# Three edits to a two-layer adaptive transformer on one core: tokens issued before weights, an output projection moved into the next row, a softmax scale moved to ScalarE

## The chip, the cores and the metric

The kernel runs on one core of a Trainium2 chip. Its time is the device time of one execution in microseconds. Before the change the median of three runs is 4261.57 us (4254.47 to 4265.86). All data are float32 except a few small helper tiles.

## The reference

Input `x` has 8 rows of 512 tokens with 256 channels. Cut to what matters, it goes through four residual branches:

```python
x = x + ssm(adaln(x))          # layer 0: a gate from eight causal averages, then a selective state-space scan
x = x + moe2(x @ W[id7] + b)   # layer 0: 8 experts, top 2, gelu, hidden 512
x = x + attention(lora_ffn(x)) # layer 1: 8 heads of width 64, values 256 wide, softmax over 512 tokens
x = x + moe4(adapter_ln(x))    # layer 1: 32 experts, top 4, swiglu, hidden 128, plus a shared expert
```

with, inside them,

```python
h = exp(dlt * A) * h + dlt * B_t * x_t        # 512 channels x 16 states, 512 steps in order
y = (C_t . h + D * x_t) * silu(z); out = y @ W_out.T
attn = softmax(Q @ K.T); out = attn @ V       # per head, summed over heads
```

In both expert layers each token goes to its best experts only, and the experts' outputs are summed with the gate's weights.

## The kernel before

A row is kept as 128 partitions x 2 halves of the channels x 512 tokens. Two Python generators write the program in turns: one for the first branch (`thread_x`), one for the second and third (`thread_y`). They yield costs, and a loop at the end lets the first advance in proportion to the second. The rows go through the second generator in four groups: row 0; rows 1 and 2; rows 3 to 5; rows 6 and 7. What is written is then ordered once more, at build time, by a list scheduler: it keeps the dependencies, takes the earlier written instruction where several are ready by its own cost figures, gives out buffers as they come free, and puts each copy written as `nc.any` on VectorE or ScalarE, whichever it holds to be free. [...]

*The scan* (`scan`, L612 to L687). A row has 64 items: 4 channel blocks `j` x 4 groups of states `g` x 4 quarters `k`. For an item ScalarE makes `dA` (L623), GpSimd `h` (L625), VectorE scans (L651) and multiplies by C (L652), and TensorE folds the states into `yp` (L660). After each channel block, VectorE adds the skip term (L664) and GpSimd multiplies by the gate into the tile `y8` (L665). When the 64 items are written, the output projection follows (L680 to L686): load the row's input as `xr`, eight products of `y8` with `W_out` into two PSUM tiles `gx` (of which there are two in all), add, store to `xa`. While the items are written, the head of the next row (gates, causal averages, convolution) is woven in by the generator's loop (L703 to L709), which then marks the row as done. Done rows let the second generator start on a group.

*The first expert layer* (L780 to L812). Tokens were scattered by GpSimd into a table in HBM, sorted by expert, in tiles of 256. For a tile, SyncE reads the expert's and the tile's numbers into registers, and issues two loads: the expert's weights `fw` (1154 KB, 4 buffers) and the tokens `xt` (260 KB, 4 buffers), the latter behind a fence on the scatters. Then TensorE transposes the tokens (L298), ScalarE copies them (L300), two products with a gelu between them follow, VectorE adds the bias into `ys` (L808), works out where the rows go (`to_m`, `to_d`, `to_i`, L306 to L310), and GpSimd scatters them (L160). Tiles are written one step apart: transposes of one, first product of the one before it, second product of the one before that.

*Attention* (L862 to L927). Per pair of heads and per 128 queries, `scores` writes the products of queries and keys, the negated maximum on VectorE (L893), the exponential with its sum on ScalarE (L896), the sum's reciprocal on VectorE (L897) and the scaling:

```python
nc.scalar.activation(ex, sp, AF.Exp, bias=nm, accum_out=den)
nc.vector.reciprocal(den, den)
nc.vector.tensor_scalar(ex, ex, den, None, ALU.mult)
```

`turn` transposes the scaled tiles on TensorE (L906) and copies them (L907, an `nc.any` copy, as are those of V at L879 and of queries and keys at L871); the products with V follow (L923).

*The last expert layer* (L1060 to L1086) has the same form as the first, with weights `mw` (384 KB), tokens of 264 KB, 7 buffers of each and 95 tiles, after everything else. A gather per row ends the program.

Of the kernel before, what the change touches and what calls it, by code (L numbers as in the profile page):

```python
# [10 lines left out]
F32 = mybir.dt.float32  # L11
# [6 lines left out]
P = 128  # L18
# [33 lines left out]
def adaln_attn_ffn_kernel(ctx: ExitStack, tc: tile.TileContext, d: dict, out: bass.AP):  # L52
# [314 lines left out]
    def thread_x(wp, wk, ps):  # L367
# [244 lines left out]
        def scan(b):  # L612

            bc3 = rows[b]
            items = [(j, g, k) for j in range(4) for g in range(4) for k in range(4)]
            yps, Cs, hs, dAs, xz = {}, {}, {}, {}, {}
            y8 = wk.tile([P, 4, T], F32, tag="y8", name="y8")

            def begin(i):
                j, g, k = items[i]  # L620
                t = got[b, j, k]
                dA = wk.tile([P, T], F32, tag="dA", name="dA", bufs=4)
                nc.scalar.activation(dA, t[:, 0, :], AF.Exp, scale=A[:, 4 * j + k, g : g + 1])  # L623
                h = wk.tile([P, T], F32, tag="h", name="h", bufs=8)
                nc.gpsimd.tensor_tensor(h, t[:, 1, :], B4s[b, g], ALU.mult)  # L625
                hs[i], dAs[i] = h, dA
                if (g, k) == (1, 0):
                    xz[j] = wk.tile([P, 2, T], F32, tag="xz", name="xz")
                    nc.sync.dma_start(xz[j], xzs[b % 2][:, j])
                if j == 0 and g < 3 and k == 1:  # L630
                    get_B4(b, g + 1)

                if j < 3 and (g, k) == (2, 3):
                    get_pack(b, j + 1, 0)
                if j < 3 and g == 3 and k < 3:
                    get_pack(b, j + 1, k + 1)
                if j == 3 and b + 1 < NB and g == 3:
                    if k == 0:
                        get_pack(b + 1, 0, 0)
                    if k < 3:  # L640
                        get_pack(b + 1, 0, k + 1)
                    if k == 3:
                        get_B4(b + 1, 0)

            def run(i):
                j, g, k = items[i]
                h = hs[i]
                if k == 0:
                    Cs[0] = ps.tile([P, T], F32, tag="c4", name="c4")
                    mm(Cs[0], [(states(4 + g), bc3)])  # L650
                nc.vector.tensor_tensor_scan(h, dAs.pop(i), h, 0.0, ALU.mult, ALU.add)  # L651
                nc.vector.tensor_tensor(h, h, Cs[0], ALU.mult)  # L652

            def add(i):

                j, g, k = items[i]
                if g == 0:
                    yps[j] = ps.tile([P, T], F32, tag="yp", name="yp")
                for k in range(4):
                    nc.tensor.matmul(  # L660
                        yps[j][32 * k : 32 * k + 32, :], fold, hs.pop(i + k), start=(g == 0), stop=(g == 3))
                if g == 3:
                    y = wk.tile([P, T], F32, tag="tr", name="y", bufs=2)
                    nc.vector.scalar_tensor_tensor(y, xz[j][:, 0, :], col("D", j), yps.pop(j), ALU.mult, ALU.add)  # L664
                    nc.gpsimd.tensor_tensor(y8[:, j, :], xz.pop(j)[:, 1, :], y, ALU.mult)  # L665

            begin(0)
            begin(1)
            for i in range(64):
                if i == 58:  # L670
                    yield from after[0]
                if i < 62:
                    begin(i + 2)
                run(i)
                if i % 4 == 0 and i > 0:
                    add(i - 4)
                if i % 2:
                    yield 5
            add(60)
            x = wk.tile([P, KC, T], F32, tag="gm", name="xr")  # L680
            nc.sync.dma_start(x, d["x"][b])
            for e in range(KC):
                pt = gx()
                mm(pt, [(W_out[:, j, ts(e, P)], y8[:, j, :]) for j in range(4)])
                nc.vector.tensor_tensor(x[:, e, :], x[:, e, :], pt, ALU.add)
            nc.sync.dma_start(xa[b], x)  # L686
            yield 3  # L687

        after = [None]
        for i, c in enumerate(head_a(0)):  # L690
            if i == 14:
# [10 lines left out]

        for b in range(NB):  # L703
            after[0] = head(b + 1) if b + 1 < NB else iter(())
            for c in scan(b):
                c += next(after[0], 0)
                c += next(after[0], 0)
                yield c
            done.add(b)  # L709

    def thread_y(q, bs, ps):
        n = len(bs)
# [9 lines left out]
        with ExitStack() as ph:  # L722
# [57 lines left out]
            def expert_tile(i):  # L780
                with behind(last[-3] if i > 2 else None):
                    te = nc.sync.value_load(tiles[0:1, i : i + 1], min_val=0, max_val=E2 - 1)
                    v = nc.sync.value_load(tiles[0:1, NT + i : NT + i + 1], min_val=0, max_val=E2 * cap // TS - 1)
                    w = wk.tile([P, FW], F32, tag="fw", name="fw", bufs=4)
                    nc.sync.dma_start(w, d["fW"][bass.ds(te, 1)].rearrange("s p f -> p (s f)"))
                    xt = wk.tile([P, 2, RW2], F32, tag="xt", name="xt", bufs=4)
                    last.append(load_after(
                        f, xt.rearrange("p j f -> p (j f)"), tabv[bass.ds(v, 1)].rearrange("s p f -> p (s f)")))
                yield 0
                xT = tokens_in(wk, acc, xt, 2)  # L790
                yield 1
                h = wk.tile([P, FC, TS], F32, tag="h", name="h2")
                for hh in range(2):
                    pt = g()
                    for i2 in range(2):
                        fc = 2 * hh + i2
                        mm(pt[:, ts(i2, TS)],
                           [(w[:, 512 * k + P * fc : 512 * k + P * (fc + 1)], xT[:, k, :]) for k in range(KC)])
                    for i2 in range(2):
                        fc = 2 * hh + i2  # L800
                        nc.scalar.activation(h[:, fc, :], pt[:, ts(i2, TS)], AF.Gelu, bias=w[:, 2304 + fc : 2305 + fc])  # L801
                yield 4
                py = acc()
                for j in range(2):
                    mm(py[:, ts(j, C)],
                       [(h[:, fc, ts(j, P)], w[:, 1024 + C * fc : 1024 + C * (fc + 1)]) for fc in range(FC)])
                ys = wk.tile([P, 2, C], F32, tag="ys", name="ys", bufs=3)
                nc.vector.tensor_tensor(ys, py.rearrange("p (j c) -> p j c", j=2), rep(w[:, 2048:2304], 2), ALU.add)  # L808
                tokens_out(wk, xt, ys, teb[:, i : i + 1], K2, tok, n * T * K2, f"tok2_{q}")
                yield 4  # L810
# [4 lines left out]
        with ExitStack() as ph:  # L815
            wk = ph.enter_context(tc.tile_pool(name=f"k3_{q}", bufs=1))
            H = 8
            for r, b in enumerate(bs):
# [43 lines left out]
                for hp in range(H // 2):  # L862
# [20 lines left out]
                    def scores(i):  # L883

                        sps = [g() for u in range(2)]

                        for u in (1, 0):
                            r0 = 64 * u
                            mm(sps[u], [(qk[r0 : r0 + 64, 0, ts(i, P)], qk[r0 : r0 + 64, 1, :])])
                        for u in range(2):  # L890
                            sp = sps[u]
                            nm = wk.tile([P, 1], F32, tag="nm", name="nm", bufs=4)
                            nc.vector.tensor_reduce(nm, sp, AX.X, ALU.max, negate=True)  # L893
                            ex = wk.tile([P, T], F32, tag="ex", name="ex", bufs=NEX)
                            den = wk.tile([P, 1], F32, tag="den", name="den", bufs=4)
                            nc.scalar.activation(ex, sp, AF.Exp, bias=nm, accum_out=den)  # L896
                            nc.vector.reciprocal(den, den)  # L897
                            nc.vector.tensor_scalar(ex, ex, den, None, ALU.mult)  # L898
                            exs[i, u] = ex

                    def turn(i):
# [100 lines left out]
    with ExitStack() as ph:  # L1002
# [57 lines left out]
        def expert_tile(i):  # L1060
            with behind(last[-5] if i > 4 else None):
                te = nc.sync.value_load(rows[0:1, i : i + 1], min_val=0, max_val=E4 - 1)
                v = nc.sync.value_load(rows[0:1, NT + i : NT + i + 1], min_val=0, max_val=E4 * CAP4 // TS - 1)
                w = wk.tile([P, 768], F32, tag="mw", name="mw", bufs=7)
                nc.sync.dma_start(w, d["mW"][bass.ds(te, 1)].rearrange("s p f -> p (s f)"))
                xt = wk.tile([P, 2, RW4], F32, tag="xt", name="xt", bufs=7)
                last.append(load_after(
                    f, xt.rearrange("p j f -> p (j f)"), tab4v[bass.ds(v, 1)].rearrange("s p f -> p (s f)")))
            yield 1
            xT = tokens_in(wk, ps_tile, xt)  # L1070
            yield 1
# [130 lines left out]
```

## Time and profile before

| | us |
|---|---|
| median of the runs | 4261.57 |
| the profiled execution | 4252.41 |
| its span, first to last instruction | 4250.6 |
| TensorE busy | 3440.5 |
| VectorE busy | 2670.9 |
| ScalarE busy | 1672.2 |
| GpSimd busy | 1565.8 |
| mean granted TensorE clock | 0.889 of full speed |

The profile names engines PE (TensorE products), PEld (TensorE weight loads), DVE (VectorE), ACT (ScalarE), POOL (GpSimd) and SP (SyncE, which issues the loads); "q" after a name is the engine's sequencer. Busy times come from one execution. [...] A line of the list of waits tells that an engine stood idle ahead of an instruction and what ended that; idle time of an engine that nothing waits for costs nothing. Scan rows end (last VectorE scan) at 395, 718, 1047, 1393, 1738, 2064, 2579 and 2903 us; the first-layer expert tiles of the four groups lie at about 482 to 655, 1149 to 1380, 2188 to 2390 and 3135 to 3279; the last layer's run from 3827 to about 4160, and the gather ends the span.

### The profile page before, as it was taken

How to read it: one execution, taken by the hardware profiler on the slowest of the kernel's cores; microseconds unless marked ns; L12 is line 12 of the kernel's file. 1: busy time of each engine (PE TensorE's matmuls, PEld its weight loads, DVE VectorE, ACT ScalarE, POOL GpSimd, SP SyncE). 2: the span in 40 equal slices, each digit the busy share in tenths (PEclk: the TensorE clock that was granted, in tenths of full speed). 3: DMA queues.
4: the chain of work that ended last, by engine and by line, in shares of the span. 5: the costliest groups of instructions: out<-in, count | busy, mean ns of one | idle time of the engine just before them, and what ended most of it. 6: DMA issues, size and time to landing. Idle time of an engine off the chain costs nothing. (4 is left out here: it accounts for less than half of the span.)

```text
span 4250.6 us, 36891 instructions
## 1 busy us (share of the span) xinstructions
PE 3440.5 (81%) x10964; PEld 1694.3 (40%) x10964; DVE 2670.9 (63%) x4290; ACT 1672.2 (39%) x2741; POOL 1565.8 (37%) x1222
## 2 busy tenths in 40 slices
PE   4556686887687888888758899889988999978994
PEld 2111352332254233333327443333456444436773
DVE  4698957886966686796892547575432454443336
ACT  2535463455366346445433443242223233322222
POOL 0456535434635333433542323231043111134552
PEclk7677798988798898999879999899989999989996
DMA  3235455324456423333346312213043312117776
GB/s 105 101 108 180 187 162 170 106 98 156 177 176 209 135 102 118 134 122 109 139 165 234 122 63 77 68 36 104 15 163 136 93 41 70 36 50 245 248 237 224
DMA packets 159372, 554.78 MB, mean 131 GB/s; under 512 B 27730, under 2 KB 34289, under 8 KB 146756
## 3 DMA queue, kind: packets, MB, share of 16 engines
q1 hardware_dynamic: 135076, 501.35, 35.2%
q0 software_dynamic: 24096, 51.08, 3.3%
q8 instruction: 87, 1.43, 0.1%
q14 instruction: 113, 0.93, 0.1%
HBM read 453.00 MB, written 234.82 MB: 162 GB/s over the span
## 5 line engine op out<-in xcount | busy, mean ns | idle before, releaser
L625 POOL TENSOR_TENSOR h<-packed,B 128x512 f32<-128x512 f32 x512 | 792.5, 1570 | 1054.2 <-PE yp L660 746.7
L651 DVE TENSOR_TENSOR_SCAN h<-dA,h 128x512 f32<-128x512 f32 x512 | 791.0, 1571 | 126.3 <-ACT dA L623 67.2
L623 ACT ACTIVATE dA<-packed,Aexp 128x512 f32<-128x512 f32 x512 | 359.8, 720 | 656.4 <-DVE h L651 446.5
L160 POOL DMA_INDIRECT tok<-ys,to_i x310 | 311.9, 1006 | 497.9 <-DVE ys L808 237.7
L660 PE MATMUL yp<-h,fold 128*32 128x512 f32 x1024 | 349.7, 704 | 156.9 <-DVE h L652 140.6
L923 PE MATMUL acc<-aT,V 128*128 128x512 f32 x1024 | 453.4, 597 | 5.3 <-ACT aT L907 3.2
L160 POOL DMA_INDIRECT tab<-row,si x192 | 197.4, 1028 | 465.5 <-issue 210.5
L652 DVE TENSOR_TENSOR h<-h,c 128x512 f32<-128x512 f32 x512 | 330.5, 672 | 29.0 <-PE c L78 28.2
L923 PEld LDWEIGHTS acc<-aT,V 128*128 128x128 f32 x1024 | 193.2, 191 | 245.9 <-issue 235.1
L78 PE MATMUL acc<-wv,c 128*128 128x512 f32 x512 | 270.2, 642 | 0.4
L78 PE MATMUL g<-qk 64*128 64x512 f32 x512 | 210.7, 681 | 54.9 <-ACT ex L896 28.6
L896 ACT ACTIVATE ex<-g,nm 128x512 f32<-128x512 f32 x256 | 173.8, 684 | 157.5 <-DVE nm L893 157.3
L78 PE MATMUL g<-xT,fw 128*128 128x256 f32 x960 | 233.6, 396 | 2.5 <-ACT h L801 1.9
L893 DVE TENSOR_REDUCE nm<-g 128x1 f32<-128x512 f32 x256 | 165.0, 681 | 100.8 <-PE g L78 100.8
L78 PE MATMUL acc<-fw,h 128*128 128x256 f32 x960 | 221.6, 383 | 3.5 <-DVE ys L808 1.8
L78 PEld LDWEIGHTS g<-xT,fw 128*128 128x128 f32 x960 | 188.0, 201 | 39.4 <-issue 6.8
L78 PEld LDWEIGHTS acc<-fw,h 128*128 128x128 f32 x960 | 182.7, 192 | 41.6 <-issue 12.4
L906 PE MATMUL acc<-ident,ex 128*128 128x128 f32 x1024 | 160.3, 286 | 47.9 <-DVE ex L898 16.2
L906 PEld LDWEIGHTS acc<-ident,ex 128*128 128x128 f32 x1024 | 122.6, 146 | 188.4 <-issue 69.3
L660 PEld LDWEIGHTS yp<-h,fold 128*32 128x32 f32 x1024 | 44.7, 115 | 364.1 <-DVE h L652 208.3
L479 DVE TENSOR_TENSOR_SCAN tr<-alpha,gm 128x512 f32<-128x512 f32 x128 | 181.4, 1435 | 5.0 <-POOL y L665 3.5
L78 PE MATMUL g<-xT,mw 128*128 128x256 f32 x760 | 183.1, 385 | 0.0
(280 smaller groups left out, 5458.3 us busy)
## 6 DMA issues: line engine op xcount, KB each, us to landing
fw<-in_fW SPq DMA_DIRECT2D x60, 1154.0 KB
tab<-zeros SPq DMA_DIRECT2D x32, 2112.0 KB
packed<-pack SPq DMA_DIRECT2D x128, 512.0 KB
mw<-in_mW SPq DMA_DIRECT2D x95, 384.0 KB
tab<-zeros SPq DMA_DIRECT2D x16, 2080.0 KB
xt<-tab SPq DMA_DIRECT2D x95, 264.0 KB
xz<-xzs SPq DMA_DIRECT2D x32, 512.0 KB
pack<-dd SPq DMA_DIRECT2D x32, 512.0 KB
```

The costliest lines, as they stand in the source:

```text
L78: nc.tensor.matmul(o, lhsT, rhs, start=(i == 0), stop=(i == len(pairs) - 1))
L160: i = nc.gpsimd.indirect_dma_start(out=table_, out_offset=bass.IndirectOffsetOnAxis(ap=idx, axis=0), in_=src, in_offset=None, bounds_check ...
L479: nc.vector.tensor_tensor_scan(tr, alpha[:, 1 + i : 2 + i].to_broadcast([P, T]), gm[:, k, :], 0.0, ALU.mult, ALU.add)
L623: nc.scalar.activation(dA, t[:, 0, :], AF.Exp, scale=A[:, 4 * j + k, g : g + 1])
L625: nc.gpsimd.tensor_tensor(h, t[:, 1, :], B4s[b, g], ALU.mult)
L651: nc.vector.tensor_tensor_scan(h, dAs.pop(i), h, 0.0, ALU.mult, ALU.add)
L652: nc.vector.tensor_tensor(h, h, Cs[0], ALU.mult)
L660: nc.tensor.matmul(yps[j][32 * k : 32 * k + 32, :], fold, hs.pop(i + k), start=(g == 0), stop=(g == 3))
L893: nc.vector.tensor_reduce(nm, sp, AX.X, ALU.max, negate=True)
L896: nc.scalar.activation(ex, sp, AF.Exp, bias=nm, accum_out=den)
L906: nc.tensor.transpose(tp[:, m, :], ex[:, ts(m, P)], ident)
L923: nc.tensor.matmul(ys[k], V[:, m, C * u + P * k : C * u + P * (k + 1)], aTs[u][:, m, :], start=(u == 0 and m == 0), stop=(u == 1 and m == 3))
```

## The change

There are three edits. In both expert layers the tokens are issued before the weights:

```diff
-                    w = wk.tile([P, FW], F32, tag="fw", name="fw", bufs=4)
-                    nc.sync.dma_start(w, d["fW"][bass.ds(te, 1)].rearrange("s p f -> p (s f)"))
                     xt = wk.tile([P, 2, RW2], F32, tag="xt", name="xt", bufs=4)
                     last.append(load_after(
                         f, xt.rearrange("p j f -> p (j f)"), tabv[bass.ds(v, 1)].rearrange("s p f -> p (s f)")))
+                    w = wk.tile([P, FW], F32, tag="fw", name="fw", bufs=4)
+                    nc.sync.dma_start(w, d["fW"][bass.ds(te, 1)].rearrange("s p f -> p (s f)"))
...
-                w = wk.tile([P, 768], F32, tag="mw", name="mw", bufs=7)
-                nc.sync.dma_start(w, d["mW"][bass.ds(te, 1)].rearrange("s p f -> p (s f)"))
                 xt = wk.tile([P, 2, RW4], F32, tag="xt", name="xt", bufs=7)
                 last.append(load_after(
                     f, xt.rearrange("p j f -> p (j f)"), tab4v[bass.ds(v, 1)].rearrange("s p f -> p (s f)")))
+                w = wk.tile([P, 768], F32, tag="mw", name="mw", bufs=7)
+                nc.sync.dma_start(w, d["mW"][bass.ds(te, 1)].rearrange("s p f -> p (s f)"))
```

A row's output projection is written after the first items of the next row's scan instead of at its own row's end; the last row's stays behind its scan. The row counts as done when its projection has been written, the head of the row after next is woven in from the third turn on, and `y8` is taken when the first channel block is finished:

```diff
-            y8 = wk.tile([P, 4, T], F32, tag="y8", name="y8")
...
                 if g == 3:
+                    if j == 0:
+                        ys8[b % 2] = wk.tile([P, 4, T], F32, tag="y8", name="y8")
+                    y8 = ys8[b % 2]
...
                 if i < 62:
                     begin(i + 2)
+                if i == 2 and last:
+                    last.pop()()
                 run(i)
...
             add(60)
-            x = wk.tile([P, KC, T], F32, tag="gm", name="xr")
-            nc.sync.dma_start(x, d["x"][b])
-            for e in range(KC):
-                pt = gx()
-                mm(pt, [(W_out[:, j, ts(e, P)], y8[:, j, :]) for j in range(4)])
-                nc.vector.tensor_tensor(x[:, e, :], x[:, e, :], pt, ALU.add)
-            nc.sync.dma_start(xa[b], x)
-            yield 3
-
+            yield 0
+
+            def project():
+                x = wk.tile([P, KC, T], F32, tag="gm", name="xr")
+                nc.sync.dma_start(x, d["x"][b])
+                for e in range(KC):
+                    pt = gx()
+                    mm(pt, [(W_out[:, j, ts(e, P)], ys8[b % 2][:, j, :]) for j in range(4)])
+                    nc.vector.tensor_tensor(x[:, e, :], x[:, e, :], pt, ALU.add)
+                nc.sync.dma_start(xa[b], x)
+                done.add(b)
+
+            last.append(project)
+
+        last, ys8 = [], {}
...
-            for c in scan(b):
-                c += next(after[0], 0)
-                c += next(after[0], 0)
+            for i, c in enumerate(scan(b)):
+                if i > 1:
+                    c += next(after[0], 0)
+                    c += next(after[0], 0)
                 yield c
-            done.add(b)
+        last.pop()()
+        yield 3
```

The exponentials of the attention are scaled on ScalarE:

```diff
                             nc.vector.reciprocal(den, den)
-                            nc.vector.tensor_scalar(ex, ex, den, None, ALU.mult)
+                            nc.scalar.activation(ex, ex, AF.Identity, scale=den)
```

As the change is built, the scheduler's choices move along: of the `nc.any` copies of attention, VectorE has 176 where it had 121 (of 448), and ScalarE's order holds 299 loads of function tables where it held 286.

## The prediction

> **What bounds the kernel now.** I read the shares of the engines first, then the stretches of time, because an average over 4250 us hides stages with different limits. Columns of the second fence: stretch, length, busy us of each engine (instructions), granted TensorE clock, DMA share, GB/s.
>
> ```profile
> PE 3440.5 (81%) x10964; PEld 1694.3 (40%) x10964; DVE 2670.9 (63%) x4290; ACT 1672.2 (39%) x2741; POOL 1565.8 (37%) x1222
> ```
>
> ```profile
> 0.00:410.00 410.00, 232.16 (x419) 64.07 (x421) 306.47 (x314) 168.82 (x217) 176.13 (x121) 0.73 0.37 122
> 410.00:2940.00 2530.00, 2063.30 (x6317) 947.09 (x6313) 1798.24 (x2457) 1144.31 (x1822) 1019.30 (x725) 0.89 0.38 132
> 2940.00:3840.00 900.00, 821.28 (x2674) 428.78 (x2675) 382.25 (x943) 252.94 (x485) 185.48 (x185) 0.95 0.25 83
> 3840.00:4160.00 320.00, 288.21 (x1427) 233.73 (x1426) 124.33 (x448) 86.33 (x179) 171.14 (x176) 0.99 0.76 240
> 4160.00:4251.00 91.00, 35.50 (x132) 20.65 (x131) 59.59 (x130) 19.80 (x40) 13.70 (x15) 0.59 0.63 231
> ```
>
> There are five stages. Until 410 row 0 of the scan runs alone, led by VectorE (75% busy). From 410 to 2940 scan rows 1 to 7 are woven with the expert layer and attention of rows 0 to 5: TensorE is 82% busy, VectorE 71%, and neither is full; [...] From 2940 to 3840 (rows 6 and 7 with the last routing) TensorE is 91% busy and simply the limit. From 3840 the 95 last expert tiles run at 90% TensorE. The tail is the gather. So time can be won at TensorE's waits, most of all in the woven stage. The third fence is the list of waits: who waited for whom, us in total, times, longest.
>
> ```profile
> PE acc L298 <- DMA xt<-tab: 48.2, 22, 9.0
> PE gx L78 <- POOL y L665: 24.4, 8, 8.5
> PE acc L906 <- DVE ex L898: 16.2, 11, 5.1
> DVE to_m L306 <- DMA xt<-tab: 178.4, 32, 14.8
> SPq L785 <- DVE ys L808: 355.6, 43, 21.4
> ```
>
> TensorE waits 48.2 us for tokens and 24.4 us for the gated scan output ahead of the output projection; VectorE stands 178.4 us in front of the tokens. The timeline of one steady first-layer expert tile shows how the token wait arises (start, length, engine, line, idle before):
>
> ```profile
> 3166.43 0.69 DVE L808 TENSOR_TENSOR ys<-acc,fw 128x512 f32<-128x512 f32 x1
> ...
> 3167.25 0.34 SPq L785 DMA_DIRECT2D fw<-in_fW  x1
> ...
> 3167.78 0.33 SPq L179 DMA_DIRECT2D xt<-tab  x1
> ...
> 3173.69 0.22 DVE L306 SCALAR_TENSOR_TENSOR to_m<-xt,sc_teb 128x4 f32<-128x4 f32 x1 [6.57 <-DMA xt<-tab]
> ...
> 3173.80 0.63 PE L298 MATMUL acc<-ident,xt 128*128 128x128 f32 x4 [0.27 <-DMA xt<-tab]
> ```
>
> It is a ring: `ys` frees a weight buffer (3167.12), weights and tokens are issued, the tokens land 5.9 us after their issue because 1154 KB go first, and the transposes, the next `ys` and the next release follow. It turns in 7.8 us; TensorE's work for a tile is 3.62 + 3.62 + 0.63 = 7.87 us of modelled spans, so ring and engine are about equal. The waits at a row's end and the scaling:
>
> ```profile
> 1062.45 3.78 PE L78 MATMUL gx<-y,W_out 128*128 128x512 f32 x4 [8.47 <-POOL y L665]
> ```
>
> ```profile
> L898 DVE TENSOR_SCALAR ex<-ex,den 128x512 f32<-128x512 f32 x256 | 161.8, 634 | 3.3
> ```
>
> ```profile
> L623 ACT ACTIVATE dA<-packed,Aexp 128x512 f32<-128x512 f32 x512 | 359.8, 720 | 656.4 <-DVE h L651 446.5 <-DMA packed<-pack 132.2 <-issue 15.1
> ```
>
> [...]
>
> **The change, part by part.** The profiled execution took 4252.4 us, 1.8 more than its span; the median is 4261.6, 9.2 above it. Sums are made against 4252.4 and moved up by 9.2.
>
> *Tokens before weights, first layer (60 tiles).* The same two transfers change places. The tokens' buffer is freed by `to_m` and the transposes, long before `ys` frees the weights'. So tile i+1's tokens go out right behind tile i's weights, about one tile (7.8 us) earlier than they are needed, and leave the ring. The weights come 0.5 to 1 us later, and TensorE wants them only one step after the transposes (the first product follows the transposes of the next tile), so 7.9 us of TensorE work hides them; if that cover were gone, each tile would lose about 1 us, 60 in all. Late next is TensorE itself. Of the 48.2 us, 8.4 lie in the last group (3135 to 3280), where nothing else can fill TensorE: worth 8 in full. The other 40 lie in the woven stage, where TensorE's freed time is partly taken by other waits: I count half, 20. Bounds: 8 and 48, and something beyond for VectorE's 84 us of token waits in the first groups, behind which scans queue. SyncE's wait for `ys` (355.6 us) stays, with the scan's loads behind it as before.
>
> *Last layer (95 tiles).* With 7 buffers nothing waits for tokens in the steady stage; its 31.8 us of TensorE idle follow VectorE's `to_i`, which waits for scatters and keeps its place in the order. Only the start gains: the first transposes wait 15.3 us, and the second tile's tokens stand behind two weight loads (384 KB each, some 1.2 us at the 319 GB/s between 1414 KB in 6.4 us and 648 KB in 4.0 us). Worth 2 us, bounds 1 and 4. A fence now holds back the first weights too, but they left only 0.6 us before the first tokens.
>
> *Projection in the next row.* No instruction is added: 16 TensorE passes, 2 VectorE adds, one load and one store per row move behind the start of the next scan. They used to sit at TensorE's head waiting for the last product on GpSimd: 24.4 us over 8 waits, and both `gx` banks were held meanwhile, so the next row's B broadcast queued behind (at 1062 to 1066). In the changed order two broadcasts come first. I take half, 12; bounds 0 and 24. No wait is added: y8 is complete by the place where the projection now stands. Row results come two scan steps later (about 10 us), but a group's expert work starts behind earlier work of the same thread, except the first group: a loss of at most 5, inside the bound. The load and store stay in SyncE's queue at nearly the same place.
>
> *Scale on ScalarE.* Removed: 256 x 634 ns = 162 us of VectorE. Added: 256 x 720 = 184 us of ScalarE. The free copies move in answer: 55 more of them fall to VectorE (680 ns each, 37 us) and leave ScalarE (586 ns, 32 us), and ScalarE gets 13 more table loads (17 us). Net VectorE -125, ScalarE +169. After 2940 TensorE covers both. In the woven stage two effects oppose. VectorE is relieved of 78 (160 of the 256 scaled tiles lie before 2940) of its 1798 us, and TensorE waits for VectorE's scan products there: a gain of up to 60. Against it, the scale now waits on ScalarE for a reciprocal that stands in VectorE's queue; in the built order two exponentials are followed by two scales, so from the trace's times of exponential and reciprocal I work out some 70 us of new standing on ScalarE in this stage, with `dA` and the copies queued behind, and VectorE's scans and TensorE behind those. And the first half's chain grows by the other exponential (0.885 with its sum read) plus 720 - 634: about 1 us. Price between -60 and +79 (worked out under the rivals); I take 0, as the two have about one size.
>
> Sum: -28 - 2 - 12 + 0 = -42; 4252.4 - 42 = 4210, and 4219 on the median's level.
>
> **The rivals.**
> - *VectorE's relief counts.* With tokens and scales gone VectorE no longer holds the scans; the list has 140.6 us of TensorE waiting for `h` of L652. A gain of 60 on top: 4219 - 60 = 4159. For it: VectorE is 71 to 75% busy there. Against: 446.5 us of `dA` waiting for scans say that ScalarE has room, but TensorE at 82% does not have much.
> - *Everything hidden.* The scheduler already weaves row ends (the next scan starts 0 to 14 us after the last) and expert tiles; TensorE's order, not the waits, sets the length: 4262.
> - *ScalarE holds the scan* (slower). The place is the woven attention of rows 0 to 5. About 40 of 160 scaled tiles there have their transposes within 0.4 us of the scale's end; at 1.1 us each that is 44, and half of the 70 us of standing reaching `dA` and the scans is 35: +79, against -42 gives +37: 4299. It decides once more than 42 us of the new standing reach TensorE. For it: `DVE h` already waits 67 us for `dA`. Against: `dA` runs two items ahead of its scan.
>
> **How the numbers follow.** Likeliest 0.52 at 4219 (its own range 4190 to 4246); relief 0.19; hidden 0.12; ScalarE 0.17. Faster by over 0.3% (a measurement of this kernel tells about 0.3% from nothing), below 4249: 0.51 + 0.19 + 0.02 = 0.72. Within: 0.01 + 0.09 + 0.01 = 0.11. Slower, above 4274: 0.01 + 0.16 = 0.17. The range 4150 to 4290 leaves out the far part of the relief (0.07) and most of the ScalarE case (0.11).
>
> **What would show it.** Right: TensorE's wait for `xt` in `acc` falls below 12 us and VectorE's below 60; tokens in the steady tiles land a tile before their transposes; the 8 waits for GpSimd's `y` shrink below 12; the stretch to 2940 shortens by some 30 us, the last one hardly. ScalarE's scale shows 0.72 us and an idle before it, for `den`, of 40 to 100 us. Wrong: `DVE h` waiting for `dA` above 120 us, or TensorE's waits for the scaled tile above 50, with the woven stage no shorter; or a static order that lets one thread run ahead and leaves a hole elsewhere.

## The result: 1.7% slower

After the change the median is 4331.77 us (4330.44 to 4338.8). The kernel before had 4258.68 us in the same comparison, so the ratio is 1.0173, with an interval of 1.0154 to 1.0192. The prediction was 4219 us. Chips differ: the unchanged kernel has medians from 4238 to 4276 us in the comparisons below, so results are given as ratios to it on the same chip.

The profiled execution took 4330.8 us with a span of 4329.1, 78.5 longer than before. Its line of busy times:

```profile
PE 3484.1 (80%) x10964; PEld 1708.7 (39%) x10964; DVE 2557.3 (59%) x4087; ACT 1815.9 (42%) x2957; POOL 1601.3 (37%) x1222
```

Work moved as intended: VectorE has 114 us less, ScalarE 144 more. TensorE has the same 10964 products and is busy 44 us longer. The stretches of the changed kernel (columns as for the kernel before; the borders are moved to the ends of its own stages):

```profile
0.00:410.00 410.00, 232.00 (x414) 63.41 (x414) 280.49 (x309) 163.09 (x211) 168.11 (x120) 0.70 0.36 119
410.00:3000.00 2590.00, 2096.57 (x6303) 955.40 (x6304) 1743.84 (x2336) 1248.57 (x1972) 1061.28 (x727) 0.88 0.38 130
3000.00:3906.00 906.00, 825.74 (x2664) 425.53 (x2663) 348.57 (x856) 295.93 (x552) 186.47 (x185) 0.95 0.22 75
3906.00:4240.00 334.00, 297.19 (x1469) 246.34 (x1470) 126.59 (x463) 89.42 (x184) 173.97 (x180) 0.97 0.77 240
4240.00:4329.00 89.00, 32.64 (x117) 17.98 (x115) 57.84 (x124) 18.88 (x38) 11.43 (x13) 0.58 0.64 236
```

The loss lies in the second line, the woven stage. The places of equal work, read from the trace, say when it came: the last VectorE scan of row 2 ends 6 us earlier than before (1040.8), that of row 5 is 35 later (2099.3), that of row 6 is 62 later (2640.4), and the last group's first tokens are issued 64 later (3200.1). From there to the last layer 15 us more are added (3906.6, +79); the last layer and the gather give none back (span end +78). The list of waits of the changed kernel:

```profile
DVE to_i L310 <- DMA tok<-ys,to_i: 398.9, 111, 11.3
DVE to_m L306 <- DMA xt<-tab: 49.0, 14, 12.7
PE acc L298 <- DMA xt<-tab: 43.9, 7, 10.2
DVE h L650 <- ACT dA L622: 34.4, 11, 8.0
PE gx L78 <- POOL y L667: 21.4, 7, 7.7
PE acc L918 <- ACT ex L910: 6.5, 5, 3.4
```

VectorE's wait for tokens fell as hoped, from 178.4 to 49.0 us. But its wait of `to_i` for scatters (L310) grew from 198.4 to 398.9 us: by stretches, 225 us of it stand in the four groups of the first expert layer, where it had 3 before, and the rest in the last layer. TensorE's wait for tokens (43.9, was 48.2) and for GpSimd's `y` (21.4, was 24.4) hardly moved. `h` waits less for `dA` than before (34.4, was 67.2). In the list of groups, the scale and `dA`:

```profile
L622 ACT ACTIVATE dA<-packed,Aexp 128x512 f32<-128x512 f32 x512 | 360.0, 719 | 601.4 <-DVE h L650 344.6
L910 ACT ACTIVATE ex<-ex,den 128x512 f32<-128x512 f32 x256 | 176.7, 720 | 37.0 <-DVE den L909 36.4
```

The scale takes 720 ns, as priced from the 720 of `dA` before, and waits 36.4 us for its reciprocal. VectorE's 398.9 us are more than the loss, but idle time of VectorE costs only where something waits for it, and no wait of TensorE's products grew by more than 26 us (the largest growth is a wait for ScalarE's `sz` in the head, 38.9 where it was 12.8). No single wait of TensorE is the loss.

### The profile page after: what moved, and what is told of

Read it like the earlier page. It is cut to its first block, busy times and chain, and to the rows that moved or that the text cites. A ratio compares the mean times of both kernels' runs of the same rounds, so it can differ in the third digit from the quotient of the medians.

```text
span 4329.1 us, 36771 instructions
## 1 busy us (share of the span) xinstructions
PE 3484.1 (80%) x10964; PEld 1708.7 (39%) x10964; DVE 2557.3 (59%) x4087; ACT 1815.9 (42%) x2957; POOL 1601.3 (37%) x1222
## 5 line engine op out<-in xcount | busy, mean ns | idle before, releaser
L624 POOL TENSOR_TENSOR h<-packed,B 128x512 f32<-128x512 f32 x512 | 813.1, 1613 | 921.4 <-PE yp L659 579.3
L650 DVE TENSOR_TENSOR_SCAN h<-dA,h 128x512 f32<-128x512 f32 x512 | 803.7, 1597 | 105.6 <-POOL h L624 68.8
L659 PE MATMUL yp<-h,fold 128*32 128x512 f32 x1024 | 373.5, 717 | 153.9 <-DVE h L651 144.4
L78 PE MATMUL acc<-wv,c 128*128 128x512 f32 x512 | 281.7, 668 | 7.2 <-DVE aT L919 2.8
L310 DVE TENSOR_SCALAR to_i<-to_d 128x2 int32<-128x2 f32 x155 | 33.3, 215 | 420.6 <-DMA tok<-ys,to_i 398.9
L910 ACT ACTIVATE ex<-ex,den 128x512 f32<-128x512 f32 x256 | 176.7, 720 | 37.0 <-DVE den L909 36.4
```

What stands on the lines that cost most here:

```text
L78: nc.tensor.matmul(o, lhsT, rhs, start=(i == 0), stop=(i == len(pairs) - 1))
L659: nc.tensor.matmul(yps[j][32 * k : 32 * k + 32, :], fold, hs.pop(i + k), start=(g == 0), stop=(g == 3))
L910: nc.scalar.activation(ex, ex, AF.Identity, scale=den)
```

## The experiments

### One part of the change at a time

Each part alone, and the whole without the scale. The core of each edit:

```diff
 only_tokens      tokens issued ahead of weights in both expert layers
-                    nc.sync.dma_start(w, d["fW"][bass.ds(te, 1)].rearrange("s p f -> p (s f)"))
...
+                    nc.sync.dma_start(w, d["fW"][bass.ds(te, 1)].rearrange("s p f -> p (s f)"))
 only_project     the projection written at item 2 of the next scan, and
-            for c in scan(b):
+            for i, c in enumerate(scan(b)):
+                if i > 1:
 only_scale
-            nc.vector.tensor_scalar(ex, ex, den, None, ALU.mult)
+            nc.scalar.activation(ex, ex, AF.Identity, scale=den)
 no_scale         only_tokens and only_project together
```

> The kernel before with the first edit alone: tokens issued ahead of weights in both expert layers. Theory A (the scale on ScalarE costs the time): the tokens' own gain is left, 4215 to 4255, with VectorE's wait for the tokens below 60 us. Theory B (the new wait for scatters in front of to_i takes the place of the old one): to_i waits some 350 to 400 us for scatters as in the changed kernel, against 198, and the time stays within 10 us of before. Theory C (any edit that moves the static order costs by chance): it may land anywhere, 4230 to 4320.

> The kernel before with the second edit alone: a row's output projection written in the next row's scan. Theory A: 4240 to 4265, as the waits for the gated product went from 24.4 to 21.4 us only. Rival: the later projection holds the next group and its rows, and this edit alone gives 30 us or more of the 73, 4290 or more. The built order holds 302 loads of function tables against 286, 16 x 1.28 = 21 us more of ScalarE, which should not count if ScalarE has room.

> The kernel before with the third edit alone: exponentials scaled on ScalarE. Theory A (this edit is the loss): 4310 to 4345, with the time lost between the end of one group's expert tiles and the next routing, where rows 1 to 5 are attended (1380 to 2085 and 2395 to 2640 of the kernel before), and TensorE's waits for ex of the exponential at 40 us or more against 29.8. Theory C: no stage stands out. If tokens and projection are the loss: 4240 to 4270.

> The first two edits without the third. Theory A: 4200 to 4250, the loss gone. If the first two are the loss: 4300 to 4330. If the three only lose together, by chance of the order: about 4260, and the third alone as well.

| | ratio to before | interval |
|---|---|---|
| only_tokens | 1.0080 | 1.0063 to 1.0098 |
| only_project | 1.0248 | 1.0231 to 1.0265 |
| only_scale | 1.0048 | 1.0031 to 1.0064 |
| no_scale | 1.0264 | 1.0238 to 1.0291 |
| the whole change | 1.0173 | 1.0154 to 1.0192 |

Each part alone loses, and the projection's part loses more than the whole change. So the theory that the scale is the loss falls. The effects do not add either: the three alone sum to +3.8%, the whole has +1.7%. The scale even changes its sign: alone it costs 0.5%, added to the other two it takes 0.9% off (no_scale against the whole change).

On the scale, the list of waits of only_scale shows that ScalarE did stand for reciprocals (51.6 us over the span, where the prediction had worked out some 70 for the woven stage), and that the scan's wait for `dA` hardly grew (75.1 us against 67.2 before):

```profile
DVE h L651 <- ACT dA L623: 75.1, 17, 10.2
ACT ex L898 <- DVE den L897: 51.6, 50, 4.6
```

### What the tokens ran into

In the third group the answer is plain. First the kernel before, then only_tokens, each with the two waits of VectorE between 2190 and 2450 us that bear on it:

```profile
DVE to_m L306 <- DMA xt<-tab: 58.6, 11, 7.3
DVE to_i L310 <- DMA tok<-ys,to_i: 0.8, 1, 0.8
```

```profile
DVE to_i L310 <- DMA tok<-ys,to_i: 102.1, 14, 10.4
DVE to_m L306 <- DMA xt<-tab: 3.5, 2, 2.4
```

A wait of 59 us for tokens went, and one of 102 us for scatters came. The timeline of only_tokens shows what stands behind it (start, length, engine, line, idle before):

```profile
2285.44 3.72 PE L78 MATMUL acc<-fw,h 128*128 128x256 f32 x16 [1.19 <-DVE ys L808]
...
2288.75 0.98 POOL L160 DMA_INDIRECT tok<-ys,to_i  x1 [2.12 <-issue]
...
2295.71 0.17 DVE L310 TENSOR_SCALAR to_i<-to_d 128x2 int32<-128x2 f32 x1 [10.32 <-DMA tok<-ys,to_i]
2295.81 0.69 DVE L808 TENSOR_TENSOR ys<-acc,fw 128x512 f32<-128x512 f32 x1
...
2296.63 0.34 SPq L788 DMA_DIRECT2D fw<-in_fW  x1
...
2296.78 0.97 POOL L160 DMA_INDIRECT tok<-ys,to_i  x1 [7.04 <-DVE to_m L306]
...
2298.06 0.98 POOL L160 DMA_INDIRECT tok<-ys,to_i  x1 [0.30 <-issue]
2306.41 0.17 DVE L310 TENSOR_SCALAR to_i<-to_d 128x2 int32<-128x2 f32 x1 [9.59 <-DMA tok<-ys,to_i]
2307.68 0.22 DVE L306 SCALAR_TENSOR_TENSOR to_m<-xt,sc_teb 128x4 f32<-128x4 f32 x1 [1.09 <-DMA xt<-tab]
...
2308.01 0.69 DVE L808 TENSOR_TENSOR ys<-acc,fw 128x512 f32<-128x512 f32 x1
2308.82 0.33 SPq L788 DMA_DIRECT2D fw<-in_fW  x1
```

Here is a second ring. `ys` lets GpSimd scatter its tile (2296.78 and 2298.06); VectorE's wait for them ends 8.3 us after the second issue; only then is one of the four `to_i` buffers free, and `to_i` of a later tile may be written (2306.41). That `to_i` stands in VectorE's queue ahead of the next `ys` (2308.01), which frees a weight buffer (2308.82) and feeds the next scatter. From `ys` to `ys` it is 12.2 us here, 1.1 of them a wait for tokens, where the ring of tokens turned in 7.8. How much of that is the ring's differs from cycle to cycle. The product for the `ys` at 2295.81 was done at 2289.16 (first line: start and length), so this `ys` stood 6.6 us behind `to_i`; the product for the one at 2308.01 was done only at 2305.55, and there `to_i` held it up by 0.9. Over the third group a tile takes 10.2 us in only_tokens against 9.4 before, over the last 9.2 against 8.6. In the kernel before, tokens came late enough that the scatters were done (`to_i` waits 0.8 us for them in this group).

So the buffers of `to_i` were raised, which takes the wait's reason away, with early tokens and without:

```diff
-        di = pool.tile([P, 2], I32, tag="to_i", name="to_i", bufs=4)
+        di = pool.tile([P, 2], I32, tag="to_i", name="to_i", bufs=8)
```

> Tokens ahead of weights in both layers, nothing else, and 8 buffers instead of 4 for the row indices that a scatter reads. Theory B (tokens are early, so VectorE's row indices come up in its order while the scatter of four tiles before still runs, and that wait takes the place of the one removed): VectorE's waits of to_i for scatters in the groups at 1150 to 3360 fall from some 200 us to under 40, and the time is at or below before, by 0 to 30 us. Rival (the loss with tokens is an accident of the order): the wait goes, but the time stays 20 to 40 us above before.

> The kernel before with 8 buffers instead of 4 for the row indices that a scatter reads, nothing else. If those buffers hold the last layer in any order of the loads, it gains what the run with early tokens and 8 buffers gained there, 30 to 40 us, and the groups stay as before: 25 to 45 us below before. If the gain came from early tokens and more buffers together: within 12 us of before.

With early tokens and 8 buffers (tokens_toi8) the ratio is 0.9931 (0.9905 to 0.9957): from 0.8% slower to 0.7% faster, and below both kernels of this case. With 8 buffers alone (toi8) it is 0.9979 (0.9964 to 0.9993). VectorE's waits for tokens and scatters in tokens_toi8 between 2190 and 2450 us, and those of its whole span:

```profile
DVE to_m L306 <- DMA xt<-tab: 66.0, 12, 13.6
```

```profile
DVE to_m L306 <- DMA xt<-tab: 156.1, 39, 13.6
DVE to_i L310 <- DMA tok<-ys,to_i: 86.7, 48, 3.8
```

The waits of `to_i` in the groups are gone, all 86.7 us that are left lie in the last layer. This was expected, and so was the time. But the line of `to_m` shows what was not foreseen: VectorE waits for tokens again, 66.0 us in the third group (58.6 before) and 156.1 in all. In only_tokens that wait was small because VectorE stood for scatters instead. In the profile of tokens_toi8 the groups only reach what they were before (the last group's first tokens are issued at 3139.3 us, 3135.7 before). Most of the gain lies in the last layer, whose tiles take from 3822.5 to 4134.6 us, 312 us, instead of 347 (3827 to 4174); the three kernels of the same chip that have the last layer as before took 337 to 341. So the buffers of `to_i` bear on the last layer too. How much is to be had there is not settled: toi8 took 333 us, and two later kernels with the last layer of tokens_toi8 took 335, on another chip (342 to 348 with four buffers there), with 239 GB/s moved instead of 256 and the same granted clock of 0.98.

### What the projection's part did

That part holds two edits. They were parted: the late head alone, and the moved projection with the head as before.

```diff
 head_late             (the kernel before, and)
-            for c in scan(b):
+            for i, c in enumerate(scan(b)):
+                if i > 1:
 project_head_now      (only_project, and)
-                if i > 1:
```

> The kernel before with one edit: the head of the next row is woven in from the third turn of the scan on; the projection stays at its row's end. Theory H (the later head crowds the end of every scan row): slower by 50 to 100 us, items 1 to 16 of a row some 10 to 15 us shorter than before and items 48 to 64 some 20 us longer. Rival R (moving the projection itself is the loss): within 15 us of before.

> The projection moved into the next row's scan as in the change, but the head of the row after next is woven in from the first turn on, as before; tokens and scale as before. Theory H: within 20 us of before, with a small gain of 0 to 12 possible (the waits for GpSimd's y). Rival R: slower by 70 to 105 us, as with the whole projection edit.

The late head alone has 1.0233 (1.0206 to 1.0260), nearly all of only_project's 1.0248. The moved projection alone has 1.0090 (1.0065 to 1.0115). The head theory holds, and the projection still loses, where its expectation allowed at most 20 us. The wait that it was to remove did go: TensorE's wait for `y` in project_head_now, from its list of waits between 395 and 3177 us, against 24.4 before:

```profile
PE gx L78 <- POOL y L667: 4.7, 3, 2.5
```

What it lost instead is the start of what follows. Measured as the start of the store of an attention row (`xb`) against the end of the scan row nearest to it, the second generator runs later by 8 to 26 us from the first attention row on (attention row 0 is stored 20.0 us later than before where scan row 2 ends 11.9 later; row 5 is stored 41.0 later where the last scan ends 30.7 later). A row counts as done only when its projection is written, so the expert and attention work of its group is written later too, and after the last scan that lag has nothing to hide behind. That is a reading of the trace; no run took this lag away. The edit also takes 3 off the cost that a row reports to the pacing loop, of 269 that the loop reckons with; a change of 1 in that number had no effect (below), one of 3 was not tried.

The same removal from the whole change, then the removal of both causes, then that without the projection:

```diff
 all_head_now          (the whole change, and)
-                if i > 1:
 all_head_now_toi8     (and)
-        ... name="to_i", bufs=4)
+        ... name="to_i", bufs=8)
 tokens_scale_toi8     tokens_toi8 and the scale on ScalarE, projection and head as before
```

> The whole change, but the next row's head woven in from the first turn as before. If the late head is the largest part of the loss, the time is 50 to 85 us below the whole change (1.0173 of before), so between 0.997 and 1.006 of before. If the late head only cost time without the scale on ScalarE: still over 1.012.

> The whole change with both suspected causes taken away: head from the first turn, 8 buffers of row indices. Theory (late head plus ring of row indices are the whole loss): 0.98 to 0.995 of before. Rival (moving the projection or the scale still holds a loss of its own): 0.995 to 1.005, behind the run with early tokens and 8 buffers alone (0.9931).

> Early tokens, the scale on ScalarE and 8 buffers of row indices; projection and head as before. If the scale costs what it did alone (+0.5 per cent), 0.998 of before. If it is worth what the whole change showed against the one without it (-0.9 per cent), 0.984. Beside the run with all three edits and both causes removed it tells what moving the projection is worth by itself.

| | ratio to before | interval |
|---|---|---|
| the whole change | 1.0173 | 1.0154 to 1.0192 |
| all_head_now | 1.0013 | 1.0001 to 1.0025 |
| all_head_now_toi8 | 0.9940 | 0.9923 to 0.9956 |
| tokens_scale_toi8 | 1.0019 | 1.0006 to 1.0031 |

Two lines of code, the head's delay, are 1.6 of the 1.7%. The 8 buffers take another 0.7% off, of which half (12 us) falls in the last layer, where `to_i` waited before the change too. The version without both causes lies at the edge of what the theory allowed, below 0.995, and is no better than tokens_toi8 with one edit of the three. The scale added to tokens_toi8 seems to cost 0.9%. But the two ran on different chips, and 23 us of the 37 between them lie in the last layer, which has no scaled tile; what the scale does in that order is not shown.

### Is it the order by itself?

A control: one pacing number by which the two generators take turns, and nothing else.

```diff
-XROW, YROW, YGROUP, YTILE, P4ROW = 269.0, 242.0, 20.0, 9.0, 10.0
+XROW, YROW, YGROUP, YTILE, P4ROW = 268.0, 242.0, 20.0, 9.0, 10.0
```

> The kernel before with one pacing number changed by 0.4 per cent (the cost of a scan row, 269 to 268, by which the two generators take turns): no work is added, removed or moved on purpose, only the written order shifts a little. If the order's chance is small beside the effects studied, within 15 us of before; if the order alone is worth tens of us, 20 to 60 us either way, and then the +0.8 per cent of the tokens and +0.5 of the scale are no more than that.

It has 1.0004 (0.9992 to 1.0016). On the way row 5's scan ends 19 us later than before, and that is made up by the end. So one small reshuffle was worth nothing at the end; the 2% of the late head are more than that.

Then the head's rhythm itself. Its 44 steps go two to a turn of two items in the kernel before, and end at about item 44 of 64.

```diff
 head_late_fast: from the third turn on, three steps a turn (ends at about item 33)
 head_fast: from the first turn on, three steps a turn (item 30)
 head_late1: from the second turn on, two steps a turn (item 46)
 head_even: from the first turn on, two steps and one by turns (item 57)
 tokens_toi8_head_fast: tokens_toi8 with three steps a turn
 all_toi8_late_fast: the whole change, 8 buffers, three steps a turn from the third on
```

> The kernel before with the head woven in from the third turn on, but three steps to a turn instead of two, so that its 44 steps end at about item 33 of the scan instead of 48 (44 before). If it is the late end of the head that costs (its chain of activations, GpSimd steps and stores runs into the last items of the row): the loss of the late head (2.3 per cent) goes, within 20 us of before. If it is the empty start of the row: still 60 to 100 us above before.

> The kernel before with three steps of the head to a turn from the first turn on, ending at about item 30. If an earlier end of the head is worth something to the row's last items: 0 to 30 us below before. If an even spread of the head over the row is what counts: 10 to 50 us above before, since the last 30 items then have no filler.

> Early tokens with 8 buffers of row indices (0.9931 of before) and three steps of the head to a turn. It follows the run with the fast head alone: 0.986 to 0.993 if the fast head gains, over 0.996 if it loses.

> The whole change with 8 buffers of row indices and three steps of the head to a turn, still from the third turn on. If the head's late end was the loss: 0.985 to 1.0 of before. If its late start was: over 1.005 (the whole change has 1.0173, the buffers take about 0.7 per cent).

> The kernel before with the head woven in from the second turn on, two steps to a turn: half of the delay. If the loss grows with the delay (each turn without filler at the row's start, each step pushed to its end): 30 to 65 us above before. If the loss is an accident of one order: anywhere, with 0 as likely as 90.

> The kernel before with the head from the first turn on, by turns two steps and one, so that it ends at about item 57 instead of 44. If the late end of the head costs: over 100 us above before, more than with the head two turns late (which ended at item 48). If what costs is a stretch of the row without filler, beside one with too much: at or below before, by 0 to 40 us.

| | ratio | stretch | TensorE busy in it | TensorE idle | clock |
|---|---|---|---|---|---|
| before | 1 | 2741 | 2257 | 484 | 0.90 |
| pace | 1.0004 | 2746 | 2275 | 471 | 0.89 |
| head_late | 1.0233 | 2842 | 2325 | 517 | 0.88 |
| head_late1 | 1.0276 (1.0253 to 1.0300) | 2856 | 2297 | 559 | 0.88 |
| head_even | 1.0237 (1.0215 to 1.0259) | 2846 | 2299 | 547 | 0.88 |
| head_fast | 1.0284 (1.0257 to 1.0311) | 2856 | 2285 | 571 | 0.88 |
| head_late_fast | 1.0156 (1.0126 to 1.0187) | 2799 | 2268 | 531 | 0.89 |
| the whole change | 1.0173 | 2810 | 2304 | 506 | 0.88 |
| all_head_now | 1.0013 | 2746 | 2277 | 469 | 0.89 |

The stretch, in us, runs from the end of row 0's scan to the first tokens of the last group: the same work in every row of the table. "Idle" is the stretch less the busy time. The profiles are of several chips: toi8, with the head as before, has 2752 on the one of head_fast, head_late_fast and all_head_now, so differences of some 10 us tell nothing. For three of them, the lines from which these numbers are (before, head_late, the whole change):

```profile
395.00:3136.00 2741.00, 2256.91 (x6908) 1036.15 (x6908) 1905.58 (x2741) 1194.53 (x1931) 1043.86 (x748) 0.90 0.37 127
```

```profile
389.00:3231.00 2842.00, 2324.59 (x6919) 1050.63 (x6919) 1936.54 (x2763) 1208.97 (x1933) 1080.26 (x753) 0.88 0.36 123
```

```profile
389.00:3199.00 2810.00, 2303.76 (x6924) 1049.51 (x6921) 1840.78 (x2591) 1324.46 (x2117) 1092.02 (x752) 0.88 0.36 125
```

tokens_toi8_head_fast has 1.0223 (1.0194 to 1.0253) and all_toi8_late_fast 1.0118 (1.0092 to 1.0145): no better version came of it. Every other rhythm of the head that was tried loses 1.6 to 2.8%, earlier or later, denser or sparser. So neither a late end (head_fast ends earliest and loses most) nor a late start (head_even and head_fast start at once), nor an uneven spread (head_even) explains it alone, and the loss does not grow with the delay: one turn costs no less than two. Three of my theories fell here. Nor do loads of function tables explain it: ScalarE has 286 of them before, 290 to 297 in head_late, head_late1 and head_even, but 274 in head_fast, which loses most.

What the slower rhythms share is the clock. The clock records of the traces hold two values in this stretch, 1.0 and 0.5. The kernel before spends 573 us at 0.5 and pace 584; the five other rhythms spend 631 to 703 there, while the time at 1.0 is 2141 to 2168 us in all seven. So what they lose is, to within 30 us, added time at half clock. This does not make the clock the first cause: all_head_now has 625 us at 0.5 without losing, and in the kernel before TensorE was busy for 32% of the 4 us ahead of a fall on the mean, against 82% of the stretch (last section), so the time at half clock may itself follow from gaps; what opens the gaps is another question.

What the rhythm changes within a row can be seen from the trace, as the mean us that rows 1 to 5 take for each eight items of the scan, from the start of a VectorE scan to the start of another:

```
items          0-8   8-16  16-24  24-32  32-40  40-48  48-56  56-64   row
before        41.1   54.5   37.3   30.9   55.1   70.9   26.1   19.3   335.3
head_late     33.8   55.2   41.3   35.8   44.8   69.2   44.0   23.8   347.8
head_fast     43.0   67.6   37.8   86.6   35.1   28.9   28.7   20.0   347.9
head_even     39.7   42.1   47.5   33.6   38.7   38.6   57.1   48.1   345.5
whole change  35.5   52.7   42.2   34.2   42.6   63.9   47.1   21.1   339.3
```

With the late head the first eight items of a row run 7 us quicker, having less beside them, and items 48 to 56, into which the end of the head moves, take 18 us more. There VectorE stands idle for 10 us a row instead of 1 (3.8 of it for an exponential of the attention), and GpSimd 4 for the head's logarithm. The longer rows are made of many waits of a few us, on all engines. One wait of TensorE is longer in every run with another rhythm of the head: the products of the feed-forward part ahead of the attention wait 21 to 35 us for `hi`, ScalarE's ReLU, in these ten runs, and 4 to 18 us in the ten with the head as before (10.4 in the kernel before). That is some 15 of the 100 us. Which of the dependences makes the two-step rhythm fit is not settled.

## Why the prediction was wrong

**Where the time goes** was read rightly. The loss, as the gain was to, lies in the woven stage, and the last layer's 345 us (347 before) hardly moved. That agrees with the 2 us forecast there but cannot confirm them, as four-buffer last layers differ by 10 us between profiles. The 15 us that came between the last group and the last layer are probably not the change's. From the last `ys` of that group to the last layer, the eight kernels that ran on the chip of toi8 take 565 to 574 us, whatever their edits, and the ten on three other chips 544 to 549; the profile of before has 548, that of the change 566.

**Tokens before weights** (predicted -30 with the last layer; measured +0.8%, some 34 us). The first ring was read rightly for TensorE in the steady tiles. In the tile that the prediction shows, the packets of the weights run from 3168.20 to 3172.34 us and those of the tokens start only at 3171.87, 4.1 us after their issue; in only_tokens TensorE waits for tokens 5 times instead of 22, four of these at the first tile of a group. But the sum did not fall below the 12 us named (38.8, was 48.2; 43.9 in the whole change), because those first waits grew from 12 to 24 us and one of 15 came, which the prediction had not priced. VectorE's wait fell below the 60 us named, to 52.5 and 49.0, for another reason than the one given, as tokens_toi8 shows with 156.1. The step that failed is "Late next is TensorE itself". Late next was `to_i`, four buffers, on the engine that also makes `ys`. The prediction saw `to_i` wait for scatters in the last layer and left it there; that the same wait comes into the first layer, as soon as the tokens are early, was to be read from the same four buffers. With 8 buffers, which alone give -0.2%, the edit measures -0.7%, 29 us of 4242. That this is the size forecast is luck: it lies mostly in the last layer, where 2 us were forecast because `to_i` "keeps its place in the order".

**The projection** (predicted -12, at worst 0; measured +2.5%). "No instruction is added", and what moves is 16 passes, 2 adds, a load and a store: this sum priced one of two edits. The head's delay by two turns, in the same part of the diff, has no term in it: it was put at nothing without a reason. It alone is +2.3%, and this is the largest step that failed. The bound of 5 us for later row results was too small as well: the second generator ran 8 to 26 us later against the scan, which is the likely reason that the moved projection alone loses 0.9% even though it takes 20 of the 24 us of waiting away.

**The scale** (predicted 0, between -60 and +79): +0.5% alone, some 20 us, inside the bounds. Alone, relief of VectorE gave nothing: in only_scale it is busy 61 us less in the stretch of the table above (1844.7 against 1905.6), and the stretch is 15 us longer. Beside the other two edits the scale took 0.9% off, so the rival of VectorE's relief is refuted for the order of the kernel before and not for every order. The rival that ScalarE holds the scan ended on the right side for a wrong reason: `h` waits 34 us for `dA`, half of before, not over 120.

**The whole.** The warning sign that came true was the last one named, an order that leaves a hole elsewhere; it had no price and no chance of its own. The prediction treated the written order as a carrier of waits that can be taken off one by one. The runs show parts that depend on each other's order: the sum of the parts (+3.8%) is not the whole (+1.7%), and 1.6 of these 1.7% hang on two lines.

## What to carry to other kernels

When a transfer is brought forward, follow the tile through every engine that handles it and count buffers: the next ring (here the scatter's row indices, on the queue that also frees the weights) must have room, or the old wait can come back longer under another name (in the third group here, 59 us for tokens as 102 for scatters). When a diff moves a step, price each line that changes the order, also those that seem only to accompany the move; in a program woven from two threads, the place of one thread's filler can be worth more (2.3% here) than the waits that a change sets out to remove. And take such parts one by one on the chip, since they do not add.

## What the runs showed of the hardware

*TensorE's clock and the gaps in its work.* At a clock record of 1.0 a float32 product of 128x512 (`yp`) takes 594 ns, at 0.5 it takes 1061 (medians of the kernel before). So idle time is not the whole loss: in head_late 33 us of new idle in the stretch came with 68 us of longer busy time, over the same products (6902 to 6924 of them in all rows of the table). In the stretch of the kernel before, TensorE has 44 gaps of more than 4 us, and for all of them the clock is at 0.5 at the gap's end or within 4 us after it; of 39 gaps of 2 to 4 us that holds for 34, of 47 of 1 to 2 us for 15. Of the 73 falls of the clock in the stretch, every one has a gap of more than 1 us in the 4 us ahead of it, and 36 have none of more than 4 us there; on the mean of all falls TensorE was busy for 32% of those 4 us, against 82% of the stretch. The 4 us are a length chosen for this count. Total idle alone does not set the busy time either: in pace it grew by 18 us while the idle shrank by 13.

*Scatters land later in the first expert layer than in the last.* Of the 310 scatters of the kernel before, the trace tells the landing of 77. The 30 in the first layer, beside weight loads of 1154 KB, took 6.0 us in the median from issue to landing and 9.5 at most; the 47 in the last, beside loads of 384 KB, took 4.0 and 5.4. The 8.3 us that closed the second ring in only_tokens are more than the 7.8 in which the first ring turned. Which difference between the layers makes the scatters later was not tested.
